# Layer 3's keys and values projected in layer 1's cross attention, and a fifth buffer of gathered rows in the product-key layer

## The chip, the cores and the metric

The kernel runs on one core of one Trainium2 chip, as one launch that computes a whole four-layer decoder. The core's engines run side by side and meet only at semaphores: TensorE (PE, with its weight loads, PEld), VectorE (DVE), ScalarE (ACT), GpSimd (POOL) and SyncE (SP, which here only issues DMAs). The metric is the device time of one execution in microseconds; before the change it is 2679.72 us, the median of three runs.

## The reference

An activation `x` of 8 sequences of 256 tokens and 256 channels goes through twelve blocks, each of the form `x = layernorm(x + block(x))`: layers 0 to 3, each with a self attention (or a convolution), a cross attention to a context `ctx` of 8 x 120 x 192, and a feed-forward block. Three blocks matter here.

Layer 1's cross attention has 16 heads of 16 channels. Layer 2's feed-forward is a product-key layer: each token and each of 4 heads chooses 8 keys, whose rows of a table are read:

```python
down = down_embed[indices]
up = up_embed[indices]
w = jnp.einsum('btd,bthkd->bthk', hidden_states, down)
w = jax.nn.silu(w) * jax.nn.softmax(scores, axis=-1)
experts_states = jnp.einsum('bthk,bthkd->btd', w, up)
mlp = jax.nn.silu(hidden_states @ Wg.T) * (hidden_states @ Wu.T) @ Wd.T
return mlp + experts_states
```

Layer 3's cross attention has 8 heads of 64 channels; its keys and values depend on the context alone:

```python
q = (x @ Wq).reshape(B, Sq, h, d).transpose(0, 2, 1, 3)
k = (context @ Wk).reshape(B, -1, h, d).transpose(0, 2, 1, 3)
v = (context @ Wv).reshape(B, -1, h, d).transpose(0, 2, 1, 3)
scores = jnp.einsum('bhid,bhjd->bhij', q, k) * scale
```

## The kernel before

**Staging.** All of `x` stays in SBUF, as rows `X` (16 tiles of 128 tokens) and turned as `xT`; so does the turned context `ctxT`. `build` (L2198) runs the blocks in turn. The weights of a block are loaded while the block before it runs: `load` (L112) takes one tile out of a pool, `w0` and `w1` by turns, and issues one DMA per weight on SP's queue; a `spare` stretch at the end of the tile can be asked for as working memory. A load waits on SP until the last reader of the tile's former weights is done, and what is behind it on SP waits too.

**Order.** The framework plans the order on every engine at build time: instructions are taken by their place in the program among those whose operands and buffers are free. [...] The order in the program is therefore a priority, and the traces show it mixed.

**Layer 1's cross attention.** `l1_xattn` (L718) calls `attention16` (L632) over the eight sequences. For each, `exps16` makes two sets of exponentials (ACT, L556), and between them `largest16` makes the scores of the next sequence (PE, L484) and their maxima (DVE, L501), which `lower16` turns on PE (L536) and adds to the queries (DVE, L538); `sums16` multiplies with the values (L605), and `project_out` and `turn` of the sequence before finish it (norm, L177 turns the rows). PSUM is used as eight banks by turns (`bank`, L447). The hook `ready` gives three functions per sequence, `early`, `late` and `last`; here it is unused. `choose` (L741) stores the rows to DRAM on SP and picks the experts.

**The product-key layer with layer 3's blocks.** `l2_ffn` (L1416) handles one sequence at a time. `expert_batches` (L1449) computes the gated MLP in 8 steps (L1496), then for each of two token tiles takes 32 rows per token, in groups of G = 4, into one of NR = 4 buffers by turns: four gathers on POOL (`gather_rows`, L953, an indirect DMA each), four dot products on DVE (L1480), silu on ACT (L1525), and the sum of the rows, one on DVE (L1527) and three on PE with a diagonal matrix made by ACT (L1531, L1532). The iterator `later` lays other work between these steps: the routing of the next sequence, and layer 3's convolution (`convolution_batches`, L1542) and cross attention (`context_batches`, L1609) of the one before. `context_batches` projects keys and values of the context on PE (L1631, L1633; their records carry L136, the line of the helper `mm`), copies the keys with ACT (L1635) and the values with DVE (L1636), and goes on with queries, scores, exponentials and sums. The last sequence's layer 3 work runs after the loop, beside layer 3's feed-forward, whose weights `w4` are loaded at L1440.

## Time and profile before

The three runs took 2677.69, 2679.72 and 2682.74 us. The profiled execution took 2687.66 us; its span, from first to last instruction, is 2685.9 us.

| what | over the span | layer 1's cross attention, 756 to 930 us | product-key stage, 1577 to 2440 us |
|---|---|---|---|
| length, us | 2685.9 | 174 | 863 |
| PE busy, us | 2173.3 | 143.2 | 673.6 |
| DVE busy, us | 1617.5 | 114.7 | 580.7 |
| ACT busy, us | 992.0 | 65.3 | 351.4 |
| POOL busy, us | 940.5 | 29.3 | 532.6 |
| granted PE clock | 0.884 | 0.81 | 0.88 |

A busy time is the union of an engine's records in a stretch. A group of instructions is read as: line, engine, operation, output and inputs by tile name, shape, count, busy time in us and mean duration in ns, then the idle time of the engine just before, with what ended it. The chain of waits follows the work that ended last back through what released each step; a stretch of it gives start, length and line. "issue" is time in which the profile shows no wait. "remote" (in the chain: "another core or an unknown queue") is a wait whose releaser the profile doesn't know. One product of float32 matrices shows as two PE records.

### The profile page before, as it was taken

Reading aid. Unit: us, or ns where it says so; the run is one execution under the profiler, and the core shown is the slowest. Engines: PE = TensorE matmul, PEld = TensorE weight load, DVE = VectorE, ACT = ScalarE, POOL = GpSimd, SP = SyncE. Lnnn points to the kernel's source line nnn. Section 1 sums busy time; section 2 is a strip of 40 time slices with the busy share of each in tenths; the row PEclk is TensorE's granted clock in tenths of the full one; section 3 lists DMA queues with packets and bytes.
Section 4 is the critical chain, followed back from the end, with each engine's and each line's share of the span. In section 5 each row is a group of like instructions: output and inputs, shape, how many; then the busy total and the mean of one; then the engine's idle time right before and its main releaser. Section 6 shows DMA issues by size and latency. Waiting matters only on the chain.

```text
span 2685.9 us, 41132 instructions
## 1 busy us (share of the span) xinstructions
PE 2173.3 (81%) x14481; PEld 1569.7 (58%) x14481; DVE 1617.5 (60%) x5506; ACT 992.0 (37%) x2269; POOL 940.5 (35%) x986
## 2 busy tenths in 40 slices
PE   8989789699998689767886877788888778778796
PEld 5656678455565468434454355566667656555575
DVE  4664200566667576346667875757668676654675
ACT  2332233234333442123342433343445434342563
POOL 1021221311111134433210246665566555662122
PEclk9998799799988789878997888889889889887898
DMA  2001431200010137511001021111111111120000
GB/s 84 2 1 56 181 131 57 71 1 1 1 68 13 52 95 224 147 38 32 17 1 59 1 68 48 44 45 42 41 44 43 46 43 42 51 73 14 1 12 20
DMA packets 84173, 135.05 MB, mean 50 GB/s; under 512 B 33445, under 2 KB 53045, under 8 KB 82048
## 3 DMA queue, kind: packets, MB, share of 16 engines
q0 software_dynamic: 52288, 79.27, 10.0%
q1 hardware_dynamic: 28924, 49.45, 5.6%
q10 hardware_dynamic: 2756, 3.72, 0.4%
q8 instruction: 115, 1.88, 0.3%
q14 instruction: 90, 0.74, 0.1%
HBM read 242.90 MB, written 17.70 MB: 97 GB/s over the span
## 4 chain that ended last, share of the span: by engine, by line
PE 38%; DVE 21%; issue 9%; POOL 4%; ACT 4%; another core or an unknown queue 4%; DMA 3%; POOLq 0%; ACTq 0%; DVEq 0%
PE po L1532 5%; PE pp L136 5%; PE s L136 4%; PE sc L136 4%; PE ph L136 2%; DVE low L517 2%; PE sc L484 2%; DMA xe<-xd,take 2%; PE pt L136 2%; DVE low L501 2%; PE sc L605 1%; DVE junk L1480 1%; DVE X L191 1%; PE s L1678 1%
## 5 line engine op out<-in xcount | busy, mean ns | idle before, releaser
L953 POOL DMA_INDIRECT rows<-in_l2f_table_dram,index x512 | 532.8, 1041 | 340.8 <-issue 122.0
L1532 PE MATMUL po<-rows,diag 128*128 128x256 f32 x768 | 226.8, 431 | 92.9 <-ACT diag L1531 62.1
L1480 DVE SCALAR_TENSOR_TENSOR junk<-rows,X 128x256 f32<-128x256 f32 x512 | 214.5, 419 | 57.2 <-DMA rows<-in_l2f_table_dram,index 34.1
L1532 PEld LDWEIGHTS po<-rows,diag 128*128 128x128 f32 x768 | 150.0, 209 | 144.4 <-ACT diag L1531 75.9
L136 PE MATMUL pp<-xT,w 128*128 128x256 f32 (+1 forms) x672 | 196.2, 429 | 26.8 <-issue 21.4
L592 POOL TENSOR_TENSOR aT<-sides,inv 128x256 f32<-128x256 f32 x64 | 46.8, 731 | 431.6 <-DVE sides L590 316.6
L136 PE MATMUL ph<-xeT,we 128*128 128x128 f32 x1248 | 182.7, 289 | 18.3 <-DMA we<-in_l0f_experts_dram,wrow 15.1
L136 PEld LDWEIGHTS ph<-xeT,we 128*128 128x128 f32 x1248 | 168.2, 199 | 38.6 <-DMA we<-in_l0f_experts_dram,wrow 16.4
L1531 ACT ACTIVATE diag<-ident,dots 128x128 f32<-128x128 f32 x384 | 133.8, 394 | 114.7 <-PE po L1532 51.7
L177 PE MATMUL pt<-ident,X 128*128 128x128 f32 x352 | 77.4, 337 | 116.9 <-DVE X L191 93.3
L136 PEld LDWEIGHTS pp<-xT,w 128*128 128x128 f32 x672 | 137.3, 213 | 57.5 <-issue 27.3
L178 ACT COPY xT<-pt 128x512 f32<-128x512 f32 x88 | 51.5, 587 | 302.5 <-PE pt L177 219.0
L953 POOL DMA_INDIRECT xe<-xd,take x87 | 85.2, 979 | 205.3 <-PE pt L968 80.6
L177 PEld LDWEIGHTS pt<-ident,X 128*128 128x128 f32 x352 | 49.6, 165 | 153.1 <-issue 53.1
L136 PE MATMUL py<-we,hT 128*128 128x256 f32 x496 | 129.1, 384 | 0.9 <-DVE hT L1097 0.9
L1074 DVE TENSOR_TENSOR y<-py,we 128x256 f32<-128x256 f32 x23 | 9.8, 424 | 197.6 <-PE py L136 197.6
L556 ACT ACTIVATE e<-sc 128x512 f32<-128x512 f32 (+1 forms) x154 | 81.4, 601 | 103.0 <-PE sc L484 73.9
L1068 ACT ACTIVATE hT<-ph,we 128x128 f32<-128x128 f32 x184 | 65.8, 367 | 119.6 <-PE ph L136 84.9
L484 PE MATMUL sc<-kv,qv 32*128 32x128 f32 (+2 forms) x1448 | 104.2, 320 | 1.7 <-DVE qv L694 0.6
L191 DVE TENSOR_SCALAR X<-z,ln_mv,rs_y 128x256 f32<-128x256 f32 x176 | 68.1, 429 | 58.8 <-POOL rs_y L147 58.4
L136 PE MATMUL s<-xT,w 128*128 128x256 f32 x256 | 72.3, 444 | 38.3 <-issue 26.4
L484 PEld LDWEIGHTS sc<-kv,qv 32*128 32x128 f32 x1448 | 80.2, 190 | 31.2 <-issue 25.9
(535 smaller groups left out, 5204.9 us busy)
## 6 DMA issues: line engine op xcount, KB each, us to landing
we<-in_l1f_experts_dram SPq DMA_DIRECT2D x32, 384.0 KB
yd<-y SPq DMA_DIRECT2D x32, 256.0 KB
rows<-in_l2f_table_dram,index POOLq DMA_INDIRECT x512
w<-in_l2x_w_dram SPq DMA_DIRECT2D x1, 4096.0 KB
yd<-y SPq DMA_DIRECT2D x23, 128.0 KB
X<-in_x_dram SPq DMA_DIRECT2D x8, 256.0 KB
xd<-X ACTq DMA_DIRECT2D x8, 256.0 KB
xd<-X SPq DMA_DIRECT2D x8, 256.0 KB
```

Of the source, the lines that this page charges most:

```text
L136: self.nc.tensor.matmul(out, lhsT=lhsT, rhs=rhs, start=n == 0, stop=n == last and bias is None)
L177: nc.tensor.transpose(pt[:, c, j, :], self.X[:, i0 + j * step, c * P : (c + 1) * P], self.ident)
L191: nc.vector.tensor_scalar(self.X[:, i, :], z[:, j, :], mv[:, j, 0:1], r[:, j : j + 1], ALU.subtract, ALU.mult)
L484: nc.tensor.matmul(sc[: shape[0], part], lhsT=lhsT, rhs=rhs, start=mask is None, stop=True, skip_group_check=True)
L501: nc.vector.tensor_reduce(low5[:, r, :, :, 0], sc, AX.X, ALU.max, negate=True)
L517: nc.vector.tensor_reduce(low4[:, r, :, 0], sc, AX.X, ALU.max, negate=True)
L556: lambda r, sc: nc.scalar.activation(e0[m][:n0, r], sc, AF.Exp),
L953: self.nc.gpsimd.indirect_dma_start(out=out, out_offset=None, in_=table, in_offset=bass.IndirectOffsetOnAxis(ap=index, axis=0), **({} if r ...
L1068: nc.scalar.activation(hT[:, g + f, :], ph[:, f, :], AF.Gelu, bias=b1[:, g + f : g + f + 1])
L1480: nc.vector.scalar_tensor_tensor(junk, row, 1.0, self.X[:, i, :], ALU.mult, ALU.mult, accum_out=out)
L1531: nc.scalar.activation(diag, self.ident, AF.Copy, scale=dots[:, k : k + 1])
L1532: nc.tensor.matmul(po, lhsT=diag, rhs=rows[:, k, D:], start=False, stop=g + k == H * K - 2)
```

## The change

Layer 3's key and value weights are loaded with layer 1's cross attention weights. There, a function `context3`, called in the `late` place of each sequence, makes layer 3's keys and values of that sequence and stores them to two new DRAM buffers. In layer 3's cross attention two loads on SP's queue take the place of the projections and copies. The 2048 columns that the two weights had in the tile of layer 3's weights become a `spare`, used as the fifth of NR = 5 row buffers.

```diff
@@ __init__
+        self.k3 = dram.tile([B, P, 4 * SC], F32, name="k3")
+        self.v3 = dram.tile([B, SC, 8 * 65], F32, name="v3")
@@ load_l1_xattn
-        *w, spare = self.load(*((f"l1x_w{n}", 2) for n in "qkvo"), rows=("l1x_bv", "l1x_bo"), spare=16 * NT + 8)
+        *w, spare = self.load(
+            *((f"l1x_w{n}", 2) for n in "qkvo"), ("l3x_wk", 2), ("l3x_wv", 2),
+            rows=("l1x_bv", "l1x_bo"), spare=16 * NT + 8,
+        )
@@ l1_xattn
+            v3 = [work.tile([SC, 8, 65], F32, name=f"v3{n}", bufs=1) for n in range(2)]
+            for t in v3:
+                nc.gpsimd.memset(t[:, :, 64:], 1.0)
...
+            def context3(b):
+
+                ctxT = self.ctxT[:, :, b * SC : (b + 1) * SC]
+                pk = self.bank([P, 4, P])[:, :, :SC]
+                for m in range(4):
+                    self.mm(pk[:, m, :], [(wk3[:, c, m * P : (m + 1) * P], ctxT[:, c, :]) for c in range(2)])
+                kT = work.tile([P, 4, SC], F32, name="k3")
+                nc.scalar.copy(kT, pk)
+                nc.sync.dma_start(self.k3[b], kT.rearrange("p m s -> p (m s)"))
+                pv = self.bank([P, 512])
+                self.mm(pv[:SC], [(ctxT[:, c, :], wv3[:, c, :]) for c in range(2)])
+                v = v3[b % 2]
+                nc.vector.tensor_copy(v[:, :, :64], pv[:SC].rearrange("p (h d) -> p h d", d=64))
+                nc.sync.dma_start(self.v3[b], v.rearrange("p h d -> p (h d)"))
+
+            def inside(b):
+                return lambda: None, lambda: context3(b), lambda: None
+
+            self.attention16(
+                project, low, vps, [SC], False, wo, bo, work, then=choose,
+                ready=(lambda: None, lambda: None, inside),
+            )
@@ l2_ffn
-                ("l3a_win", 2), ("l3a_wout", 2), *((f"l3x_w{n}", 4 if n == "o" else 2) for n in "qkvo"),
-                rows=("l3a_bout", "l3a_ln_w", "l3a_ln_b", "l3x_bo"),
+                ("l3a_win", 2), ("l3a_wout", 2), ("l3x_wq", 2), ("l3x_wo", 4),
+                rows=("l3a_bout", "l3a_ln_w", "l3a_ln_b", "l3x_bo"), spare=8 * D,
...
+            win, wout, wq, wo, bout, ln_w, ln_b, bo, fifth = w3
...
-                experts = self.expert_batches(w, pool, work, ps)
+                experts = self.expert_batches(w, fifth, pool, work, ps)
@@ expert_batches
-        NR, G = 4, 4
+        NR, G = 5, 4
...
-        rowbufs = [pool.tile([P, G, 2 * D], F32, name=f"rows{n}") for n in range(NR)]
+        rowbufs = [pool.tile([P, G, 2 * D], F32, name=f"rows{n}") for n in range(NR - 1)]
+        rowbufs.append(fifth.rearrange("p (k d) -> p k d", k=G))
@@ context_batches
-        v1 = pool.tile([SC, 8, HD + 1], F32, name="v1")
-        nc.gpsimd.memset(v1[:, :, HD : HD + 1], 1.0)
...
             kT = pool.tile([P, 4, SC], F32, name="kT")
-            pk = ps.tile([P, 4, SC], F32, name="s")
-            for m in range(4):
-                self.mm(pk[:, m, :], [(wk[:, c, m * P : (m + 1) * P], ctxT[:, c, :]) for c in range(2)])
-            pv = ps.tile([P, 512], F32, name="s")
-            self.mm(pv[:SC], [(ctxT[:, c, :], wv[:, c, :]) for c in range(2)])
+            nc.sync.dma_start(kT, self.k3[b].rearrange("p (m s) -> p m s", m=4))
+            v1 = pool.tile([SC, 8, HD + 1], F32, name="v1")
+            nc.sync.dma_start(v1, self.v3[b].rearrange("p (h d) -> p h d", h=8))
             yield
-            nc.scalar.copy(kT, pk)
-            nc.vector.tensor_copy(v1[:, :, :HD], pv[:SC].rearrange("p (h d) -> p h d", d=HD))
```

More of the change, by code (lines that the diff above doesn't have):

```diff
@@ L719, in l1_xattn @@
         nc = self.nc
-        wq, wk, wv, wo, bv, bo = w
+        wq, wk, wv, wo, wk3, wv3, bv, bo = w
         with ExitStack() as ctx:
             work, low, vps = self.attn16_pools(ctx, "x1", SC, 1)
+            v3 = [work.tile([SC, 8, 65], F32, name=f"v3{n}", bufs=1) for n in range(2)]
+            for t in v3:
+                nc.gpsimd.memset(t[:, :, 64:], 1.0)
             bv, bo = self.everywhere(bv, work, "bv"), self.everywhere(bo, work, "bo")
@@ L754, in choose @@
                     nc.vector.max_index(self.top1_i[:, i, :], self.top1[:, i, :], lg[:, j, :])
-            self.attention16(project, low, vps, [SC], False, wo, bo, work, then=choose)
+            def context3(b):
[17 more added lines that the diff above has]
+            )
             o = 0
@@ L1421, in l2_ffn @@
             w3 = self.load(
-                ("l3a_win", 2), ("l3a_wout", 2), *((f"l3x_w{n}", 4 if n == "o" else 2) for n in "qkvo"),
-                rows=("l3a_bout", "l3a_ln_w", "l3a_ln_b", "l3x_bo"),
+                ("l3a_win", 2), ("l3a_wout", 2), ("l3x_wq", 2), ("l3x_wo", 4),
+                rows=("l3a_bout", "l3a_ln_w", "l3a_ln_b", "l3x_bo"), spare=8 * D,
             )
-            win, wout, wq, wk, wv, wo, bout, ln_w, ln_b, bo = w3
+            win, wout, wq, wo, bout, ln_w, ln_b, bo, fifth = w3
             pool3 = ctx.enter_context(tc.tile_pool(name="a3", bufs=1))
@@ L1428, in l2_ffn @@
             convolve = self.convolution_batches((win, wout, bout, ln_w, ln_b), pool3, ps3)
-            attend = self.context_batches((wq, wk, wv, wo, bo), pool3, ps3)
+            attend = self.context_batches((wq, wo, bo), pool3, ps3)
             later = iter(())
@@ L1447, in l2_ffn, with expert_batches @@
             self.fixed_point(w4, pool, work, ps)
-    def expert_batches(self, w, pool, work, ps):
+    def expert_batches(self, w, fifth, pool, work, ps):
         nc = self.nc
@@ L1611, in context_batches @@
         nc = self.nc
-        wq, wk, wv, wo, bo = w
+        wq, wo, bo = w
         HD = 64
-        v1 = pool.tile([SC, 8, HD + 1], F32, name="v1")
-        nc.gpsimd.memset(v1[:, :, HD : HD + 1], 1.0)
         half = [slice(0, HD), slice(HD, 2 * HD)]
@@ L1626, in batch @@
             )
-            ctxT = self.ctxT[:, :, b * SC : (b + 1) * SC]
             kT = pool.tile([P, 4, SC], F32, name="kT")
-            pk = ps.tile([P, 4, SC], F32, name="s")
-            for m in range(4):
-                self.mm(pk[:, m, :], [(wk[:, c, m * P : (m + 1) * P], ctxT[:, c, :]) for c in range(2)])
-            pv = ps.tile([P, 512], F32, name="s")
-            self.mm(pv[:SC], [(ctxT[:, c, :], wv[:, c, :]) for c in range(2)])
+            nc.sync.dma_start(kT, self.k3[b].rearrange("p (m s) -> p m s", m=4))
+            v1 = pool.tile([SC, 8, HD + 1], F32, name="v1")
+            nc.sync.dma_start(v1, self.v3[b].rearrange("p (h d) -> p h d", h=8))
             yield
-            nc.scalar.copy(kT, pk)
-            nc.vector.tensor_copy(v1[:, :, :HD], pv[:SC].rearrange("p (h d) -> p h d", d=HD))
             qT = pool.tile([P, 4, S], F32, name="qT3")
```

## The prediction

> **What bounds the kernel now.** I read the stretches first, to see which stages the change touches and who is busy there. Columns: length, busy time of PE, weight loads, DVE, ACT, POOL (instructions in brackets), granted clock, DMA share, GB/s.

> ```profile
> 756.00:930.00 174.00, 143.20 (x1291) 97.51 (x1290) 114.70 (x306) 65.34 (x129) 29.27 (x41) 0.81 0.08 31
> 1577.00:2440.00 863.00, 673.63 (x2990) 520.15 (x2990) 580.69 (x2856) 351.37 (x916) 532.58 (x512) 0.88 0.17 47
> ```

> The first is layer 1's cross attention, where the projections go; the second is the product-key stage with layer 3's convolution and cross attention laid into it, which they leave. In both PE is the busiest, 82% and 78%. In the second POOL is not far behind: a gather repeats every 1.30 us (1.00 of work, 0.30 before the next), so 512 of them need 667 of the 863 us however many buffers there are.

> Next the groups, kept apart by shape over 1572 to 2445, for the work that moves (count | busy, mean ns | PE idle before it):

> ```profile
> L136 PE MATMUL s<-ctxT,w 128*128 128x120 f32 x112 | 15.6, 298 | 0.0
> L136 PE MATMUL s<-w,ctxT 128*120 128x512 f32 x28 | 13.2, 593 | 0.0
> L1636 DVE COPY v<-s 120x512 f32<-120x512 f32 x7 | 4.8, 689 | 7.4 <-PE po L1532 6.7 <-PE s L136 0.7
> L1635 ACT COPY kT<-s 128x480 f32<-128x480 f32 x7 | 3.9, 559 | 24.6 <-PE po L1532 11.8 <-remote 7.3 <-PE s L136 5.5
> ```

> Seven of the eight batches run there: 28.8 us of PE, 4.11 each, with no idle time before them. They fill no hole; they stand in a queue that is moving. The chain of waits says whether that queue was the one that counted (start, length, what; pieces from several stretches):

> ```profile
> 2075.66 3.69 PE s L136 x20
> ...
> 2188.98 3.69 PE s L136 x20
> ...
> 2303.42 3.69 PE s L136 x20
> ...
> 2426.28 5.28 PE s L136 x20
> ```

> Each of these blocks of 20 is the 16 key and 4 value records of one batch, on the path whole.

> Last, the waits of the gathers and of those who read them (us, times, longest):

> ```profile
> POOL rows L953 <- PE po L1532: 93.9, 53, 6.8
> ...
> POOL rows L953 <- DVE rest L1527: 44.6, 10, 11.1
> ...
> ACT qT L1473 <- remote: 38.8, 4, 12.2
> ...
> DVE junk L1480 <- DMA rows<-in_l2f_table_dram,index: 34.1, 33, 5.0
> ```

> POOL stops 138 us for a buffer; DVE waits only 34 us for rows. "Remote" is a wait of ACT that no view explains; over the stage's seven ACT lines that show it, it comes to 134.8 us. The timeline shows one with its input long there (PE's matmul for it ended at 2200.7) while POOL goes on gathering to 2211.4:

> ```profile
> 2211.06 0.59 ACT L1473 COPY qT<-pp 128x512 f32<-128x512 f32 x1 [12.21 <-remote]
> ```

> **Part 1: projections leave the product-key stage.** On the chain: 3 x 3.69 + 5.28 + 1.38 (a piece at 1856.24) = 17.7 us. In the other two batches, at 1736 and 1968, ACT or DVE was later and nothing is saved. The copies have 3.0 us on the chain (kT twice 0.56; v 0.60, 0.60, 0.67), but both kT pieces follow a remote wait that stays; I leave them out. Behind the four blocks the next matmul on PE is the row product `po`, already waiting, so the queue closes up: **-18 us**. The eighth batch runs in the tail, 2519.7 to 2526.1, while DVE works on the convolution's norm until 2535: nothing taken, 6.6 us at most.

> **Part 2: the fifth buffer.** It lets POOL run four gathers further, 4 x 1.30 = 5.2 us, after each stop. The gain is bounded by DVE's 34.1 us less the first filling (4.5 us at 1588 to 1595, before any buffer was full): 29.6. Below it is bounded by the floor of 667 us: where no stop came before, a wait for rows stays. The chain has POOL's rows at 2.4% of 863 = 20.7 us, and arriving rows at 1883, 2177, 2379 and 2437 for 10.0 us. I take the latter: there the rows were last to arrive, each within 25 us after a stop of POOL, and 2 to 3 us are inside the 5.2. In the 20.7 us the `diag` products of ACT are next in line (PE waited 62.1 us for them), so I give them nothing: **-10 us**, ends 0 and -30. The extra fill of 2048 columns takes POOL 1.8 us like the two at 1561; POOL is idle 12.27 us before the first gather, which hides it.

> **Part 3: the projections in layer 1.** PE gets 8 x 4.11 = 32.9 us more. Where they stand, after the next batch's scores and before the turned maxima, PE waits for DVE now:

> ```profile
> PE pt L177 <- DVE X L191: 10.2, 5, 3.4
> PE pt L177 <- DVE low L501: 10.1, 3, 3.4
> ```

> With two waits of 1.4 us in the first batch that is 23 us of holes in about the right place, of PE's 30.8 idle in the 174. The longest, 3.37 us, holds most of one batch's 4.11; holes of 1.46 hold a third. I take 21 us as covered, 12 as path. Two banks of the rotation of eight are taken per batch; the bank in question was last read by the exponentials, which end within 1.5 us of the maxima's matmuls, so they fit the hole. Queued behind a late bank on PE would be the turned maxima, and DVE behind those. ACT's eight copies of 0.56 are hidden (ACT is busy 65 of 174); DVE's eight of 0.69 stand in the chain's DVE share, a third counted: 2. **+14 us**, ends +4 (the holes take nearly all; a filled hole could also hold the clock above its 0.81) and +38 (no cover, 32.9 + 5.5).

> **Part 4: DMAs.** Removed: two 512 KB loads at 1557. They were behind nothing urgent (the rows for `affine`, last in that queue, were in use at 1569.3, right after PE's own work): 0. Added: the same two behind layer 1's other weights, which are loaded at 269 to 271, beside layer 0's routing and 480 us ahead of use. At the 267 GB/s of 271 to 274 they take 3.9 us, and the DMA engines stand idle from 277 to 283: 0. SP issues 16 stores in the cross attention at about 0.43 us each; behind them are only the stores of X, first read after 937: 0. It issues 16 loads in the product-key stage; each waits for the last reader of the one buffer, a batch ahead of use, and behind it is only the next such load and, at 2399, layer 3's feed-forward weights. The last pair may come behind those 2 MB, near 2415, and is needed at 2523: 0. [...] The row: each batch moves 245 + 250 KB; at the 180 GB/s of the stretch 748 to 756 that is 2.8 us of engine time, in a stage with a DMA share of 0.17. By the row, room is plenty and I add 1 us in all. [...]

> **Sum.** -18 - 10 + 14 + 1 = -13 us against the profiled execution, 2687.66 us (span 2685.9, 1.8 around it): 2674.7. The runs' median is 2679.72, 0.3% lower, so 2666.7 on that scale: **2667 us, 0.5% faster**. No change means within 0.2%, 5.4 us.

> **Rivals.**
> *The buffer gives nothing* (consumers, not gathers, limit). For: POOL's waits are four times DVE's. Against: the four arrivals on the chain. -18 + 14 + 1 = -3: 2677, no change.
> *The fifth buffer prolongs ACT's remote waits* (the slower side). Several end as POOL stops or pauses: ACT resumes at 1604.4 (POOL out of buffers from 1602.3), 1863.4 (1862.1), 2236.0 (2234.5), 2326.3 (2325.8), 2211.1 (2211.4). If what ACT waits for is held up by the gathers, four gathers more hold it 5.2 us longer, five times: +26, so 2693. Against: waits of 8 to 11 us at 1753, 1999 and 2094 end in the middle of gathering. From -13 it takes 18 us, some four such waits, to be slower by 0.2%. [...]
> *Layer 1 hides nothing*: +38, so 2691.
> *The buffer is tied to the weights' tile*, so that gathers wait for other parts of it. Against: layer 2's attention gathers 64 times into a weight tile and waits there for its own readers (30.6 us, 4 times) only. 1%.

> **Chances.** Forecast's case, -25 to -6: 0.40; more than that, with the tail's 6.6 or 20 us and more from the buffer: 0.10; no change: 0.12; longer ACT waits: 0.23; layer 1 uncovered, or an order of instructions at large that comes out worse: 0.15. Faster 0.50, same 0.12, slower 0.38. The likeliest case alone is 2655 to 2674. The range goes up past both slow rivals and half of their sum to 2702, and down to 2640 (-18 - 24 + 4, rounded).

> **What would show it.** Right: no `ctxT` records after 1577, the stage 20 to 35 us shorter, DVE's wait for rows near 15 us, 10 to 18 us more between 756 and 930, the L177 waits there largely gone. Wrong: ACT's remote waits over 150 us; DVE's wait for rows at 30 again; or the cross attention longer by 30. Since all engines' orders are planned anew, shifts in stages that the change doesn't touch would upset the sum.

## The result, and the profile after

The changed kernel takes 2655.65 us, the median of four runs (2644.03 to 2660.45). The kernel before has 2681.23 us over its four runs (2677.69 to 2693.62). The ratio of the comparison is 0.9861, with a 95% interval of 0.9823 to 0.9899; by it the gain is 27 to 48 us, by the two medians 25.6 us, and by the two profiled executions 2687.66 - 2655.88 = 31.8 us. (The ratio is not that of the medians; with four runs each the two lie some 12 us apart, so the gain is known no better than that.) The kernel before wanders between groups of runs (2681 to 2693 us on the first chips), so from here on each kernel is compared by its ratio to runs of the kernel before on the same chip.

The two stretches that the prediction showed, in the windows view of the changed kernel (length, busy time of PE, weight loads, DVE, ACT, POOL, granted clock, DMA share, GB/s). Both are moved to the same events: from the load of layer 2's cross attention weights to the last stores of layer 1, and from the first gather to just behind the last.

```profile
758.00:927.00 169.00, 149.28 (x1457) 106.86 (x1455) 119.27 (x314) 70.36 (x138) 29.47 (x43) 0.94 0.17 58
1580.00:2398.00 818.00, 643.19 (x2833) 500.89 (x2834) 563.63 (x2815) 342.88 (x903) 535.85 (x512) 0.88 0.19 53
```

Layer 1's cross attention has 166 PE records more, and is 5 us **shorter** than the 174 us of before. The clock beside it went from 0.81 to 0.94. The product-key stage went from 863 to 818 us, 45 us less where 20 to 35 were expected.

The groups of the changed kernel in the first stretch, by shape, show the projections in their new place:

```profile
L139 PE MATMUL sc<-ctxT,w 128*128 128x120 f32 x128 | 16.4, 281 | 0.0
...
L139 PE MATMUL sc<-w,ctxT 128*120 128x512 f32 x24 | 11.3, 593 | 0.0
...
L772 ACT COPY k<-sc 128x480 f32<-128x480 f32 x8 | 4.5, 563 | 7.2 <-PE sc L139 7.2
...
L139 PE MATMUL pt<-w,ctxT 128*120 128x512 f32 x8 | 3.8, 593 | 0.0
```

Together 31.5 us of PE (32.9 were expected). Behind 1572 us no record reads `ctxT` any more, so the four blocks of the chain are gone. PE's own waits in the first stretch begin so (us, times, longest):

```profile
PE pt L180 <- DVE X L194: 3.4, 1, 3.4
PE sc L139 <- POOL aT L595: 3.2, 2, 2.9
```

L180 is the L177 of before: its 20.3 us of waits are down to 3.4. These holes were filled, as predicted; that the stage would grow by 10 to 18 us all the same did not happen.

Last the waits in the product-key stage:

```profile
POOL rows L983 <- PE po L1563: 61.3, 44, 6.2
...
POOL rows L983 <- DVE rest L1558: 27.3, 12, 7.6
...
POOL w L983 <- PE po L1563: 15.0, 9, 4.1
...
ACT qT L1504 <- remote: 14.2, 2, 11.0
...
DVE junk L1511 <- DMA rows<-in_l2f_table_dram,index: 4.1, 5, 1.1
```

`w` is the fifth buffer, which lies in the tile of the weights. DVE's wait for rows fell from 34.1 us to 4.1, below the 15 that were predicted. ACT's waits of unknown cause are still there: 127.9 us over the stage, 140.3 before (both from the first load of layer 3's weights to the first of the next, as in the table below).

### The profile page after: what moved, and what is told of

It reads as the page before. It is cut to its first block, busy times and chain, and to the rows that moved or that the text cites. A ratio compares the mean times of both kernels' runs of the same rounds, so it can differ in the third digit from the quotient of the medians.

```text
span 2654.1 us, 41230 instructions
## 1 busy us (share of the span) xinstructions
PE 2156.2 (81%) x14481; PEld 1564.3 (59%) x14481; DVE 1617.1 (61%) x5506; ACT 987.5 (37%) x2268; POOL 948.7 (36%) x988
## 3 DMA queue, kind: packets, MB, share of 16 engines
q0 software_dynamic: 52288, 79.27, 10.2%
## 4 chain that ended last, share of the span: by engine, by line
PE 47%; DVE 25%; issue 9%; DMA 6%; POOL 5%; ACT 4%; another core or an unknown queue 4%; POOLq 0%; ACTq 0%; DVEq 0%
PE sc L139 6%; PE pp L139 6%; PE ph L139 5%; PE po L1563 5%; PE s L139 3%; PE sc L487 3%; PE py L139 3%; DVE low L520 2%; DMA xe<-xd,take 2%; PE pt L139 2%; DVE low L504 2%; DVE X L194 2%; DMA we<-in_l0f_experts_dram,wrow 2%; PE s L1702 1%
## 5 line engine op out<-in xcount | busy, mean ns | idle before, releaser
L983 POOL DMA_INDIRECT rows<-in_l2f_table_dram,index x412 | 431.3, 1047 | 241.2 <-issue 107.2
L139 PE MATMUL pp<-xT,w 128*128 128x256 f32 (+1 forms) x672 | 202.7, 441 | 34.3 <-issue 23.3
L1563 PE MATMUL po<-rows,diag 128*128 128x256 f32 x618 | 177.2, 422 | 43.8 <-ACT diag L1562 20.4
L1511 DVE SCALAR_TENSOR_TENSOR junk<-rows,X 128x256 f32<-128x256 f32 x412 | 172.5, 419 | 15.6 <-remote 4.4
L139 PEld LDWEIGHTS pp<-xT,w 128*128 128x128 f32 x672 | 141.6, 219 | 66.7 <-issue 30.6
L180 PE MATMUL pt<-ident,X 128*128 128x128 f32 x352 | 74.8, 332 | 122.3 <-DVE X L194 105.2
L1563 PEld LDWEIGHTS po<-rows,diag 128*128 128x128 f32 x618 | 121.7, 207 | 79.4 <-issue 30.0
L180 PEld LDWEIGHTS pt<-ident,X 128*128 128x128 f32 x352 | 47.9, 162 | 158.7 <-issue 71.3
L983 POOL DMA_INDIRECT w<-in_l2f_table_dram,index x100 | 104.6, 1046 | 51.7 <-issue 21.6
L139 PE MATMUL sc<-xT,w 128*128 128x512 f32 x216 | 104.8, 635 | 1.4 <-ACT xT L181 1.4
```

Source lines behind the costliest of these rows:

```text
L139: self.nc.tensor.matmul(out, lhsT=lhsT, rhs=rhs, start=n == 0, stop=n == last and bias is None)
L180: nc.tensor.transpose(pt[:, c, j, :], self.X[:, i0 + j * step, c * P : (c + 1) * P], self.ident)
L983: self.nc.gpsimd.indirect_dma_start(out=out, out_offset=None, in_=table, in_offset=bass.IndirectOffsetOnAxis(ap=index, axis=0), **({} if r ...
L1511: nc.vector.scalar_tensor_tensor(junk, row, 1.0, self.X[:, i, :], ALU.mult, ALU.mult, accum_out=out)
L1563: nc.tensor.matmul(po, lhsT=diag, rhs=rows[:, k, D:], start=False, stop=g + k == H * K - 2)
```

## The experiments

The experiments came in three groups, each on one chip (e1 to e4; e5 and e6; e7 to e9). "Layer 1" is the time from the load of L2X's weights to the first expert load, "stage" the time from the first load of layer 3's attention weights to the first load of layer 3's feed-forward weights, both read from SP's timeline of the one profiled execution. "ACT remote" and "DVE for DMA" are the sums over the stage of ACT's waits without a known releaser and of DVE's waits for transfers. Two cautions go with the columns. The end mark of "stage" is a load that some orders issue earlier than others: from it to the start of the last gather it is 30 us in the changed kernel and 56 in e6 order a. And one profiled execution is one sample: in e3 ACT runs through the stage in the same order as in the kernel before, and it still took 14 us longer there.

| kernel | ratio to before (95%) | layer 1, us | stage, us | ACT remote, us | DVE for DMA, us |
|---|---|---|---|---|---|
| before | 1 | 181.1 | 843.5 | 140.3 | 30.6 |
| changed | 0.9861 (0.9823 to 0.9899) | 175.0 | 805.7 | 127.9 | 4.1 |
| e1 changed, 4 buffers | 0.9929 (0.9906 to 0.9951) | 176.4 | 843.6 | 155.3 | 15.8 |
| e2 changed, 3 buffers | 0.9837 (0.9806 to 0.9867) | 174.7 | 796.2 | 83.0 | 74.2 |
| e3 before + layer 1's part | 0.9999 (0.9981 to 1.0016) | 174.9 | 857.7 | 142.4 | 30.2 |
| e4 changed, no projections | 0.9867 (0.9833 to 0.9902) | 177.3 | 810.3 | 123.7 | 1.8 |
| e5 5 buffers, order a | 0.9974 (0.9951 to 0.9997) | 176.3 | 832.2 | 158.0 | 2.6 |
| e6 4 buffers, order a | 0.9985 (0.9964 to 1.0006) | 174.7 | 817.3 | 126.3 | 8.5 |
| e5 5 buffers, order b | 0.9837 (0.9806 to 0.9868) | 176.4 | 803.1 | 132.7 | 2.7 |
| e6 4 buffers, order b | 0.9836 (0.9806 to 0.9865) | 173.2 | 813.7 | 124.3 | 15.6 |
| e7 before, 3 buffers | 0.9965 (0.9947 to 0.9982) | 181.1 | 726.0 | 0 | 135.0 |
| e9 before, order b | 0.9983 (0.9967 to 0.9999) | 178.4 | 733.9 | 0 | 129.5 |
| e9 before, order a | 0.9992 (0.9979 to 1.0006) | 178.4 | 731.3 | 0 | 125.8 |

### The parts of the change, taken singly (e1 to e4)

**Four buffers.** Only the number is changed; the freed columns stay empty.

```diff
-        NR, G = 5, 4
+        NR, G = 4, 4
...
-        rowbufs = [pool.tile([P, G, 2 * D], F32, name=f"rows{n}") for n in range(NR - 1)]
-        rowbufs.append(fifth.rearrange("p (k d) -> p k d", k=G))
+        rowbufs = [pool.tile([P, G, 2 * D], F32, name=f"rows{n}") for n in range(NR)]
```

> The changed kernel with four row buffers instead of five; the freed columns stay unused. It holds the two moves of the projections apart from the buffer. Prediction's split: the buffer is worth 10 us, so this is 10 us slower than the changed kernel, some 2666 us. Rival 'the buffer carries most': 25 to 35 us slower than the changed kernel, 2680 to 2690, no better than before. Rival 'PE carries most': within 4 us of the changed kernel, and DVE's wait for rows is back near 30 us without costing anything.

2671.44 us, 0.9929: the changed kernel without its fifth buffer keeps 19 us of gain (0.71% of 2692.9, the kernel before in this group), and the buffer seems to be worth the rest, 0.0068 of it, 18 us. By medians it is less: the gain is 25.6 us with five buffers and 21.5 with four, each within its own group, which leaves 4 us. Taken alone and by the ratios, this run would have put the buffer between the prediction's split and the first rival.

**Three buffers.** The same edit with `NR, G = 3, 4`.

> The changed kernel with three row buffers. If buffers are worth 10 us each near this size, 10 to 20 us more than with four. If the fourth already covers nearly all and the fifth gives nothing, still 10 to 30 us more than with four, while four and five agree. If DVE's waits for rows are the term that the buffers remove, the wait grows from some 15 us (five) past 34 us (four) to 60 us or more (three).

2650.62 us, 0.9837: faster than four by 21 us, and no slower than five. Two lines of its waits, from 1560 to 2390 us:

```profile
DVE junk L1510 <- DMA rows<-in_l2f_table_dram,index: 77.3, 83, 2.9
...
ACT silu L1126 <- remote: 34.4, 7, 9.7
```

The wait for rows did what was expected of it, 74 to 77 us, eighteen times that of five buffers. The time did not follow it, so no price for a buffer can be read from that wait. Something else differs between these three kernels.

**Layer 1's part alone.** The kernel before, with the new weights loaded and `context3` called as in the change; its two results are stored and not read, and the product-key layer makes its own.

```diff
+            def inside(b):
+                return lambda: None, lambda: context3(b), lambda: None
...
-            self.attention16(project, low, vps, [SC], False, wo, bo, work, then=choose)
+            self.attention16(
+                project, low, vps, [SC], False, wo, bo, work, then=choose,
+                ready=(lambda: None, lambda: None, inside),
+            )
```

> The kernel before, with layer 3's keys and values also made and stored in layer 1's cross attention; nothing reads them, and the product-key layer still makes its own. Prediction: +14 us, so 2693 us. Rival 'cover': the added matmuls fill PE's holes and keep the granted clock up, so layer 1's cross attention is 4 to 8 us shorter with a clock above 0.9 (0.81 before), and the time is 2671 to 2681 us. Rival 'luck of the order': the stage got shorter after the change for reasons of its planned order; here it comes out 5 to 15 us longer.

0.9999, with an interval of 5 us either way: no cost, where 14 us were predicted. **The reverse** takes the projections out of the changed kernel, and leaves the transfers (`k0` and `v3` hold constants):

```diff
             def context3(b):
-                ...
+                nc.sync.dma_start(self.k3[b], k0.rearrange("p m s -> p (m s)"))
+                nc.sync.dma_start(self.v3[b], v3[b % 2].rearrange("p h d -> p (h d)"))
```

> The changed kernel without the projections in layer 1: constants are stored to the two DRAM buffers in their place, so layer 3's keys and values are left out of the computation, and all transfers stay. Prediction: 14 us faster than the changed kernel, some 2641 us. Rival 'cover': no faster, the granted clock in layer 1's cross attention falls back to 0.8 to 0.85 and its length stays at 170 us or more; 2652 to 2662 us.

0.9867 beside the changed kernel's 0.9861: without its 31.5 us of projections the kernel is no faster. The intervals of these two are 9 to 10 us either way, so e3 is the sharper of the pair. In both, ACT runs through the product-key stage in the same order as in the kernel compared with, so this test is free of the effect of the order that e5 and e6 show below. Both fit the rival "cover", which e4's expectation names. The windows view of the two over layer 1's cross attention, e3 first:

```profile
758.00:926.00 168.00, 148.32 (x1452) 106.07 (x1451) 119.24 (x314) 69.76 (x136) 29.15 (x41) 0.94 0.17 57
```

```profile
757.00:928.00 171.00, 140.27 (x1295) 95.63 (x1294) 116.20 (x306) 65.73 (x130) 30.60 (x45) 0.83 0.16 57
```

With the projections the granted clock is 0.94, without them 0.83, whether the rest of the kernel is the old or the new one. In the other profiled kernels it is the same: over 757 to 927 us the nine profiles with the projections in this stretch (e8 below among them) have 0.91 to 0.94, the five without 0.81 to 0.83. And the stretch "layer 1" is 173.2 to 177.7 us in the nine, 177.3 to 181.1 in the five without.

### The order (e5 and e6)

Each change of the number of buffers makes the framework plan the orders of PE, DVE, ACT and POOL anew. To see what that alone does, the place at which the iterator `later` is advanced is moved by one row product. Work, transfers and buffers stay.

```diff
-                        if k % 2:
+                        if k == 0:
                             next(later, None)
```

This is order a; order b has `if k == 2`. Each was run with five buffers (e5) and with four (e6).

> The changed kernel, five buffers; the iterator of other work is advanced after the first of a group's three row products instead of after the second. The work is the same; the planned orders of PE and ACT differ from the changed kernel's by some 1000 lines. Theory 'order': times of one buffer count scatter by 10 to 30 us when the order changes, so this may lie anywhere from 2645 to 2680 us and overlap with its four-buffer twin. Theory 'depth': five buffers stay some 15 us ahead of four in every order, 2650 to 2660 us.

> The same new order of advancing, with four buffers. Theory 'depth': 2665 to 2680 us, at least 10 us more than its five-buffer twin. Theory 'order': the difference to the twin is of either sign and unlike the 16 us between the first pair.

> The changed kernel, five buffers; the iterator is advanced after the third of a group's row products. Same work again, another planned order (some 400 to 700 lines). Theory 'depth': 2650 to 2660 us. Theory 'order': anywhere from 2645 to 2680 us.

> The same, with four buffers. Theory 'depth': at least 10 us more than its five-buffer twin, 2665 to 2680 us. Theory 'order': the difference to the twin is of either sign. If over the three pairs the mean difference is above 10 us and each has the same sign, the fifth buffer is worth its 10 us; if the signs differ, its worth can't be told from the order's.

Order a took 2686.38 and 2685.58 us, order b 2651.16 and 2649.50. Five against four buffers is -18 us in the order as written, then -3 us, then nothing, by the ratios (0.9861 and 0.9929; 0.9974 and 0.9985; 0.9837 and 0.9836). The order moves both by some 36 us. So the theory "depth" falls: in two of three orders the fifth buffer shows no worth outside the intervals, and the first pair's difference can't be told from the order's.

What the order acts through is not shown. In the ten profiles up to here the four longest stages, 832 to 858 us, are the four with the largest sums of ACT's unknown waits, 140 to 158 us; the other six have 83 to 133 us and 796 to 817 us. But this rests on the end mark: from the first gather to the last, e6 order a takes 850.0 us, with no more of these waits (126.3 us) than the changed kernel (127.9), which takes 815.0.

### Another chip (e7, e9, e8)

The last group was to measure the move of the projections in other orders: the kernel before with three buffers, and with the orders a and b.

```diff
-        NR, G = 4, 4
+        NR, G = 3, 4
```

> The kernel before with three row buffers instead of four; the projections stay where they were. Its twin with the projections moved took 0.9837 of the kernel before. If the move is worth 18 to 20 us in every order, this is at 0.990 to 0.992, 2665 to 2672 us. If the move is worth nothing and all is the planned order, it is at 0.98 to 0.986 like the twin. If three buffers are too few as such, above 1.0.

> The kernel before, with the iterator of other work advanced after the third of a group's row products instead of the second; nothing is moved. Its twin with the projections moved (four buffers) took 0.9836. If the move is worth 18 to 20 us in every order, this is at 0.990 to 0.992. If it is the order that gained the 42 us of the twin, it is at 0.982 to 0.986 here too. If the order scatters freely, anything from 0.985 to 1.01.

> The kernel before, with the iterator advanced after the first of a group's row products. Its twin with the projections moved (four buffers) took 0.9985. If the move is worth 18 to 20 us in every order, this is at 1.005 to 1.006, some 2705 us. If the move is worth nothing, at 0.997 to 1.0. With the other pairs (four buffers as planned: 18.5 us; order b; three buffers) the mean of the four differences is the move's worth, and their spread is the order's.

This group fell on a chip on which the kernel before takes 2566.83 us instead of 2692.9. Three buffers gave 0.9965, the orders 0.9983 and 0.9992. The pairs with the earlier runs can't be formed across such a difference, so the worth of the move in other orders stays open. What the group shows instead is the same program without ACT's unknown waits. In the kernel before, first chip, ACT's timeline at the end of a sequence (start, length, engine, line, operation; in brackets the idle time before it):

```profile
1989.48 0.20 ACT L1525 ACTIVATE dots<-dots 128x4 f32<-128x4 f32 x1 [1.38 <-DVE junk L1480]
1999.49 0.59 ACT L178 COPY xT<-pt 128x512 f32<-128x512 f32 x1 [9.81 <-remote]
```

and PE's timeline with the transposes that this copy reads:

```profile
1989.10 0.49 PE L177 MATMUL pt<-ident,X 128*128 128x128 f32 x3
```

They ended at 1989.59, and ACT began 9.9 us later, while POOL issued seven gathers. On the last chip, in order b of the same kernel, a copy of the same line near the same time comes 1.14 us after ACT was free, as soon as PE's transposes are done:

```profile
1988.15 0.59 ACT L178 COPY xT<-pt 128x512 f32<-128x512 f32 x1 [1.14 <-PE pt L177]
```

None of ACT's waits in the stage is "remote" there, nor in the other two kernels of the group. ACT is not the only engine concerned. On the first chips DVE has such waits too, 14 to 47 us of the stage in each of the ten profiles, and none on the last chip. Three times in the kernel before, the two come free within 0.2 us of each other. Here DVE's scores `s` were done on PE at 2229.2, and POOL went on gathering to 2234.5:

```profile
2235.90 1.22 DVE L1664 TENSOR_REDUCE nm<-s 128x4 f32<-128x480 f32 x2 [6.17 <-remote]
```

```profile
2236.04 0.40 ACT L1531 ACTIVATE diag<-ident,dots 128x128 f32<-128x128 f32 x1 [5.19 <-remote]
```

On the last chip the stage takes 726 to 734 us instead of 796 to 858. What DVE waits for is then the rows. The wait view of order b on that chip:

```profile
ACT dots L1525 <- DVE junk L1480: 147.0, 75, 5.6
DVE junk L1480 <- DMA rows<-in_l2f_table_dram,index: 142.3, 161, 4.0
```

The other stages take nearly the same: 472 us and less, instead of 476 to 483, from the first expert load to the load of `l2f_wq`, and 146.4 for 146.1 to 149.1 behind it. So some 110 of the 126 us between the chips lie in the product-key stage (the kernel before in its own order was timed there, but not profiled).

The last run leaves out the gathers:

```diff
-                    for k in range(G):
-                        self.gather_rows(rows[:, k, :], table, index[:, g + k : g + k + 1], 4096)
```

> The changed kernel without the 512 gathers in the product-key layer: the row buffers keep their first zeros, so the sum over the experts' rows is left out; products, sums and all else stay. It asks what ACT's waits of unknown cause hang on (128 us over the stage in the changed kernel, single ones up to 12 us). If the gathers hold something up, these waits fall below 30 us and the stage is 60 us shorter or more. If they belong to the code or its order, they stay above 80 us. In both cases POOL no longer bounds anything and PE's 640 us of work in the stage are its floor.

2407.77 us in its one run, with a stage of 581.1 us, and no unknown wait. As this chip has none with the gathers either, the run can't tell whether the gathers cause them. It does show what the gathers hold up when ACT is not held: 145 to 153 us of the stage, against the three other kernels of this group (in which the projections are in the stage too).

## Why the prediction was right, and where it was wrong

The time lies in the range, and its sign was right. Part of this is luck: the change's own gain can't be told from the gain of the order that came with it, and the same change in order a gains 7 us by the ratio (0.9974) instead of 37. By its steps:

**Part 1, -18 us: fits, though not shown apart from the order.** The change with four buffers gained 19 us, and part 3, which is also in it, costs nothing. But the stage of its one profiled execution is as long as before (843.6 and 843.5 us; from first to last gather 853.8 and 860.3), and in orders a and b the same change was 4 and 44 us ahead of the kernel before in its own order. The eighth batch, costed at nothing, gave nothing that shows: from the last gather to the end it is 259.2 us, 248.8 before.

**Part 2, -10 us: the waits went as predicted, the price is not shown.** The fifth buffer took 30 us of waits for rows away, the whole of the bound that was named. In the three pairs it was worth 18, 3 and 0 us by the ratios (4, -1 and -2 by the medians). The step that failed is "I take the latter: there the rows were last to arrive". It read a price off the waits on one chain; but three buffers, with 74 us of waits for rows, are as fast as five, and on the last chip, where ACT has no unknown waits, three buffers (0.9965) are no slower than four. That a wait for rows and a wait of ACT stand in for each other would fit e2, which has most of the one (74.2 us) and least of the other (83.0); it is not shown, since the order changed too. Part of what the gathers gain is also given back: the five-buffer kernels gather from first to last in 815.0 and 811.9 us where their four-buffer twins (order as written, order b) take 853.8 and 825.5, and then need 9.7 and 11.2 us more from the last gather to the end; in order a they gain nothing (856.8 against 850.0).

**Part 3, +14 us: wrong by its whole size, and the clearest reason why the forecast gain was too small.** The step was "I take 21 us as covered, 12 as path". Measured are 0 (0.9999, interval 5 us either way) by adding the part to the kernel before, and no gain (0.9867 to 0.9861) by taking it away. The layer's own stretch even became shorter by adding the part (181.1 to 174.9 us, e3) and longer by taking it away (175.0 to 177.3, e4).

The reason is the clock, which the prediction had only in a bracket, as part of its lower end. The two windows of the result give the account. With 31.5 us of work added, PE's busy time rose by 149.28 - 143.20 = 6.1 us, so the work that was there already took some 25 us less; PE's idle time fell from 30.8 to 19.7 us. The 21 us to be covered by holes were 11; the other 25 came from faster matmuls. The same group of matmuls, before and after, shows them (555 ns each, then 421):

```profile
L605 PE MATMUL sc<-e,vp 120*32 120x256 f32 x176 | 20.9, 555 | 0.0
```

```profile
L608 PE MATMUL sc<-e,vp 120*32 120x256 f32 x208 | 15.6, 421 | 0.0
```

The windows of 10 us of the two kernels, before first:

```profile
812.00:822.00 10.00, 6.63 (x51) 4.78 (x49) 5.27 (x17) 2.62 (x6) 1.58 (x3) 0.65 0.09 29
822.00:832.00 10.00, 10.00 (x66) 6.09 (x62) 7.40 (x23) 3.39 (x6) 1.49 (x2) 0.84 0.00 0
```

```profile
812.00:822.00 10.00, 9.59 (x98) 6.93 (x96) 8.02 (x17) 3.21 (x6) 2.17 (x3) 1.00 0.25 78
822.00:832.00 10.00, 10.00 (x78) 6.58 (x81) 7.76 (x28) 3.73 (x8) 1.46 (x2) 1.00 0.01 2
```

```profile
814.00:815.00 1.00, 0.00 (x0) 0.00 (x0) 1.00 (x4) 0.00 (x0) 0.00 (x0) 1.00 0.03 8
815.00:816.00 1.00, 0.00 (x0) 0.00 (x0) 1.00 (x3) 0.00 (x0) 0.00 (x0) 0.53 0.62 209
...
824.00:825.00 1.00, 1.00 (x9) 0.30 (x2) 0.96 (x5) 0.42 (x1) 0.00 (x0) 0.50 0.00 0
825.00:826.00 1.00, 1.00 (x5) 0.90 (x5) 0.62 (x2) 0.00 (x0) 0.73 (x1) 0.85 0.00 0
```

So this hole of 3.4 us costs PE some 5 us of clock on top of itself (an estimate: half of the 10.2 us at half clock). Read in windows of half a us, the stretch to 925 us spends 65 us at half clock before, in seven pieces of 3.4, 6.8, 10.2 or 17.1 us, and 18 us after. Shorter holes show it too, but not all of them. Of the three idle times of 1.5 us in this stretch, those that end at 796.6 and 876.1 are followed within 2 us by half clock, for 6.8 and 10.2 us, and the one that ends at 839.0 is not; what sets it apart, no view shows. A term for this was to be had from the 0.81 in the first row that the prediction quoted: 0.19 of PE's 143.2 us busy is 27 us at most (an estimate from that row), where 25 were measured.

**Part 4, +1 us: nothing against it.** No wait of the changed kernel from 1560 us to the end is put down to the loads of `kT` and `v`. No run leaves these loads out, so the 1 us stays an estimate, and what they cost the gathered rows is not measured by itself; the DMA share of the stage went from 0.17 to 0.19.

**The sum.** With part 3 at zero it is -18 - 10 + 1 = -27 us, against 27 to 48 measured by the ratio. That the two meet does not confirm parts 1 and 2: an order alone moves more than either, and the prediction gave the order no term.

**Readings.** Two of the prediction's readings are slightly off. ACT's waits of unknown cause in the stage stand in nine lines of the view, not seven, and come to 140.3 us, not 134.8. The wait that ends at 2094 took 7.4 us, so the three waits "of 8 to 11 us" took 8.1, 9.8 and 7.4. Neither enters the sum.

**The rivals.** "The buffer gives nothing" is nearest to the runs of orders a and b, though its price (2677 us) held the +14. "The fifth buffer prolongs ACT's waits" is not borne out: twice the five-buffer kernel has more of them than its twin (158.0 and 126.3; 132.7 and 124.3), once fewer (127.9 and 155.3), and the time doesn't follow the number of buffers. It had looked at the right waits: where they are missing, the stage is some 110 us shorter, far more than any part of the change. "Layer 1 hides nothing" falls with e3.

**What stays open:** how much of the stage's gain is the moved projections', how much the buffer's and how much the order's; and what ACT and DVE wait for. ACT's unknown waits happen only in stretches in which POOL gathers (in the profile of before none from 0 to 932 us, 33.3 us from 932 to 1200, 14.3 from 1200 to 1409, none from 1409 to 1556, none behind 2460), but not in all of them: POOL gathers for layer 0's experts too, before 932. The packets that the DMA view puts down to instruction queues don't go with these waits: in those of 12.2 us (to 2211.1) and 9.8 us (to 1999.5) none moves, in the one of 11.6 us (to 2326.3) one does. The program alone doesn't make these waits, as three kernels like it show none on another chip, and no view names a releaser. Whether the change gains as much on that chip wasn't tried.

## What to carry to other kernels

Before you charge added matmuls to a stage, look at the granted clock there: where PE has short holes and the clock is below 1, work that fills them can cost nothing, because the work around it speeds up. Here 31.5 us of matmuls went in at a granted clock of 0.81; it rose to 0.94, one group of matmuls went from 555 to 421 ns each, and by itself the addition left the time at 0.9999. A wait in a profile is not yet a price: change it in the other direction too (one buffer fewer), and if the time doesn't get worse, don't count on what you take away to pay by its length. Here DVE waited 74 us for rows with three buffers and 4 with five, at ratios of 0.9837 and 0.9861. Where a planner lays out the orders, run each size in two or three neutral orders before you credit a gain to it: here that alone moved the time by 36 us.

## What the runs showed of the hardware that was not expected

One and the same program took 2692.9 us on one chip and 2566.83 on another. On the chips of the first ten profiles, two at least, ACT stood without a known releaser for 83 to 158 us of the product-key stage, up to 16.5 us at a time, and DVE for 14 to 47 us, while POOL's gathers went on. On the chip of the last group there was none of it; and there the change of order or of the number of buffers moved the time by at most 0.35%, against up to 1.5% between orders on the others. And in layer 1's cross attention of the kernel before, the granted clock was at half for 3.4 to 17.1 us, seven times, beginning within 2 us of the end of a hole of 1.4 to 3.4 us on PE; at one such hole, of 1.5 us, it stayed at 1.
